# New keys' probabilities turned with the cached keys' instead of by a TensorE transpose, in an fp32 attention kernel on one core

## The chip, the core and the metric

The kernel runs on one core of a Trainium2 chip. The metric is the device time of one execution in microseconds. All arithmetic is in fp32. A core has TensorE (PE in the profile; PEld is its weight load, which overlaps the matmuls), VectorE (DVE), ScalarE (ACT), GpSimd (POOL) and SyncE (SP), each with its own instruction queue worked off in order, and 16 DMA engines.

## The reference

Four stages change a residual stream x of 32 sequences x 32 tokens x 512; the last is paged attention, and the change lies in it:

```python
x = x + L0(x, ...)   # per-sequence 32x32 mixing of tokens
x = x + L1(x, ...)   # a linear layer with a per-sequence LoRA
x = x + L2(x, ...)   # a per-sequence 512x512 linear layer
# L3: grouped-query attention, 32 query heads, 8 key heads, head size 128
k_all = concat([k_cache[block_table], k])   # 512 cached keys + the sequence's 32 new ones
scores = einsum(q, k_all) * SCALE           # cached keys at or past cache_seqlens masked
o = einsum(softmax(scores), v_all)
x = x + einsum(o, Wo)
```

## The kernel before, in words

The first part of the kernel, about a third of the time, computes L0 to L2, the projections, norms and rotations. The rest is one loop over 256 units (`for n in range(N + LAG)`), a unit being one sequence b (32) and one key head g (8), with `n = 8 b + g`. A unit is a 128-row problem: 4 query heads of the group x 32 tokens on the partitions, 544 keys (512 cached, 32 new) along the free axis. Four units make a quad, two quads (q = 0 and 1) a sequence. "Step" below means n modulo 8, counted 0 to 7; sequence b's scores are made in its own eight steps.

The order on all five engines is the order of the code (`manual_schedule`). Each step issues, in this order:

- `scores` (L1019, L1020): two pairs of matmuls on TensorE into `s_ps`, of which there is **one** buffer; then VectorE adds the mask, scales, and takes the row's minimum in one custom instruction (L1028, with an accumulator read after it), which frees `s_ps`.
- `exponentials` (L1044): ScalarE, in place in `pr` (128 x 544 for each unit, a tile for each quad), with the row sum read out after it.
- `flip_kept` (L1154): a finished quad's output is transposed by VectorE in 32x32 blocks into `ot`, one step after it was kept, but in one case in eight later (the fourth element of `kept`).
- `place`, four steps behind: the probabilities of a whole quad must be turned so that keys lie on the partitions. At step 4q + 4 + j VectorE transposes 32-column blocks of all four units at once (L1057, 128x512, into `turned`); then four copies, each from 32 partitions to 32 others (32x512), put the blocks where a 128-key chunk wants them in `placed`. ScalarE makes two of the four copies, or three in the last step of a second quad (L1069). The rest go to POOL for first quads (L1071, steps 4 to 7) and to VectorE for second quads (L1073, steps 0 to 3 of the next sequence), but for sequence 0, where POOL makes them. Two `turned` and two `placed` tiles exist.
- The new keys' 32 columns go another way. POOL gathers them from the four units in `gather_new` (L1080), at the step with j = 0; TensorE transposes the 128x128 result against the identity matrix in `flip_new` (L1084), at j = 2; ScalarE copies it out of PSUM (L1086).
- `share` (L1174): a share of the output projection of an earlier group of four sequences (a token tile t): one matmul of 128x512 (two instructions in the trace) for each unit of `SHARE`, a list of how many to issue in each of 32 steps, which starts at step 5. `LAST` is the list for the last but one tile, and takes its first 14 entries from `SHARE`. After the 32nd, VectorE adds the residual (L1183), and the projection's one PSUM buffer can be used for the next tile.
- `values`, eight steps behind (L1097): four matmuls of 128 keys into `o_ps`. After unit 3, `new_values` (L1117) adds the new keys' part for the whole sequence in eight small matmuls, and `keep` (L1131, L1133) divides the quad's output by the row sums on VectorE. After unit 7, `keep` follows for the second quad.
- After step 7, `see_keys` (L218) makes the next sequence's mask on VectorE.

Output tiles share PSUM banks: `o_ps` has one bank for each u (a unit's place in its quad), with q = 0 in its first quarter and q = 1 in its second.

Of the kernel before, what the change touches and what calls it, by code (L numbers as in the profile page):

```python
# [12 lines left out]
F32 = mybir.dt.float32  # L13
# [7 lines left out]
P = 128  # L21
B, S, HID = 32, 32, 512
D, HQ, HK = 128, 32, 8
REP = HQ // HK
PAGES, PSIZE, NPP = 64, 32, 16
L = NPP * PSIZE
# [12 lines left out]
QUAD = 4  # L39
AHEAD = 8  # L40
VS_BUFS = 2
LATE = 12
N_LOW = 9


C_BT, C_SEQ, C_TOK, C_LAB, C_COND = 0, 128, 160, 168, 176
# [13 lines left out]
def cond_resid_kernel(  # L60
# [18 lines left out]
    nc = tc.nc  # L79
# [35 lines left out]
    ident = const.tile([P, P], F32, name="ident")  # L115
# [106 lines left out]
    def load_new_keys(b: int):  # L222
        nc.sync.dma_start(out=kts[b][:, NPP, :], in_=k_d[b])
# [672 lines left out]
    tp = turn.enter_context(tc.tile_pool(name="a_t", bufs=1))  # L896
# [99 lines left out]
    ps_p = ctx.enter_context(tc.tile_pool(name="b_p", bufs=1, space=PSUM, side="right"))  # L996
# [5 lines left out]
    tp = ctx.enter_context(tc.tile_pool(name="b_t", bufs=2, side="right"))  # L1002
# [3 lines left out]
    dens, prs, pos = {}, {}, {}  # L1006
    first = L - N_LOW * PSIZE

# [3 lines left out]
    def scores(b: int, g: int):  # L1012
# [5 lines left out]
        q = qt[:, u * REP * S : (u + 1) * REP * S]  # L1018
        nc.tensor.matmul(ps[:, first:L], q, kt4[:, :N_LOW, g, :], start=True, stop=True)  # L1019
        nc.tensor.matmul(  # L1020
            ps[:, L : first + LT], q, kt4[:, N_LOW:, g, :], start=True, stop=True
        )
# [27 lines left out]
    placed = {}  # L1050

    def place(b: int, q: int, j: int):
        if j == 0:
            placed[b, q] = tp.tile([P, QUAD, L // P, P], F32, tag="placed", name=f"placed_{b}_{q}")
        pr = prs[b, q][:, :, :L].rearrange("p u (c j s) -> p j u c s", j=P // S, s=S)[:, j]
        part = tp.tile([P, QUAD, L // P, S], F32, tag="turned", name=f"turned_{b}_{q}_{j}")
        nc.vector.transpose(part, pr)  # L1057

        on_pool = q == 0 or b == 0
        if b == 0:  # L1060
            on_act = 1 + q
        else:
            on_act = 3 if q == 1 and j == QUAD - 1 else 2
        for i in range(P // S):
            dst = placed[b, q][j * S : (j + 1) * S, :, :, i * S : (i + 1) * S]
            src = part[i * S : (i + 1) * S]
            dst, src = (a.rearrange("p u c s -> p (u c) s") for a in (dst, src))
            if i < on_act:
                nc.scalar.copy(dst, src)  # L1069
            elif on_pool:  # L1070
                nc.gpsimd.tensor_copy(dst, src)  # L1071
            else:
                nc.vector.tensor_copy(dst, src)  # L1073

    pqs, pns = {}, {}

    def gather_new(b: int, q: int):

        pqs[b, q] = tp.tile([P, QUAD, S], F32, tag="pq", name=f"pq_{b}_{q}", bufs=1)
        nc.gpsimd.tensor_copy(pqs[b, q], prs[b, q][:, :, L:])  # L1080

    def flip_new(b: int, q: int):
        pnp = ps_p.tile([P, P], F32, tag="p", name=f"pn_ps_{b}_{q}")
        nc.tensor.transpose(pnp, pqs.pop((b, q)).rearrange("p u s -> p (u s)"), ident)  # L1084
        pns[b, q] = tp.tile([P, P], F32, tag="pn", name=f"pn_{b}_{q}")
        nc.scalar.copy(pns[b, q], pnp)  # L1086

    def values(b: int, g: int):

        vt = vts[b]  # L1090
        q, u = divmod(g, QUAD)
        if g == 0:
            pos[b] = ps_o.tile([P, QUAD, L], F32, tag="o", name=f"o_ps_{b}")
        po = pos[b][:, u, q * D : (q + 1) * D]
        pt = placed[b, q][:, u, :, :]
        for c in range(L // P):
            nc.tensor.matmul(  # L1097
                po,
                pt[:, c, :],
                vt[:, c, g * D : (g + 1) * D],  # L1100
                start=(c == 0 and q == 0),
                stop=(c == L // P - 1 and q == 1),
            )
        if u == QUAD - 1:
            if q == 0:
                new_values(b)
            placed.pop((b, q)), prs.pop((b, q))
            keep(b, q)

    def new_values(b: int):  # L1110

        vn = vns[b]
        for q in range(HK // QUAD):
            pn = pns.pop((b, q))
            for i in range(QUAD):
                r = slice(i * S, (i + 1) * S)
                nc.tensor.matmul(  # L1117
                    pos[b][:, i, q * D : (q + 1) * D],
                    pn[r, :],
                    vn[r, q, :],  # L1120
                    start=(q == 1),
                    stop=(q == 0),
                )

    kept = []

    def keep(b: int, q: int):

        po = pos[b] if q == 0 else pos.pop(b)
        rden = tp.tile([P, QUAD], F32, tag="rden", name=f"rden_{b}_{q}")  # L1130
        nc.vector.reciprocal(rden, dens.pop((b, q)))  # L1131
        o = tp.tile([P, QUAD * D], F32, tag="os", name=f"os_{b}_{q}")
        nc.vector.tensor_tensor(  # L1133
            o.rearrange("p (u d) -> p u d", d=D),
            po[:, :, q * D : (q + 1) * D],
            rden.unsqueeze(2).to_broadcast([P, QUAD, D]),
            ALU.mult,
        )


        at = BT * HK * (b // BT) + LAG + HK + QUAD - 2 if (b % BT, q) == (0, 1) else 0
        kept.append((b, q, o, at))
# [60 lines left out]
    LAG = 8  # L1203

    SHARE = [1, 1, 2, 1, 1, 1, 1, 1, 2, 1, 1, 1, 1, 1] + [1, 1, 0] + [1] * 7 + [0] + [1] * 7

    LAST = SHARE[:14] + [1, 1, 0, 1, 0, 1, 1, 1, 1, 1, 0, 1, 0] + [1, 1, 1, 2, 2]
    BEGIN = BT * HK + LAG - QUAD + 1  # L1210

    def share(n: int):
        t, i = divmod(n - BEGIN, BT * HK)
        if 0 <= t < NT - 1:
            parts = LAST if t == NT - 2 else SHARE
            done = sum(parts[:i])
# [4 lines left out]
    units = [(b, g) for b in range(B) for g in range(HK)]  # L1221
# [25 lines left out]
    with tc.manual_schedule(engines=order):  # L1247
        for n in range(N + LAG):
            b, g = divmod(n, HK)
            if n == FILLED + 2:  # L1250
                pa.close()
                late = ctx.enter_context(tc.tile_pool(name="b_w", bufs=1))
                places.append(late)
                wos[1] = late.tile([P, LATE, HID], F32, name="wo_1")
            if BEGIN <= n <= N and n % (BT * HK) == 0:

                load_residual((n - BEGIN) // (BT * HK))
            if n < N:
                if g == 0 and b >= 1:
                    load_queries(b, 1)  # L1260
                if g == 0 and 1 <= b < B - 1:
                    load_keys(b + 1)
                    load_new_keys(b + 1)
                    keys.dsts = page_keys(b + 1)
                    keys.transfer(slice(0, 12))
                if g < L // P and b >= 2:
                    load_value_chunk(b, g)
                if g == QUAD and b < B - 1:
                    load_queries(b + 1, 0)
                    load_inverses(b + 1)  # L1270
                    if b >= 1:
                        keys.transfer(slice(12, NPP))
                    if 1 <= b < B - 2:
                        load_table(b + 2)
                if g == QUAD + 1 and b >= 1:
                    load_new_values(b)
                if g == QUAD + 2 and b < B - 2:
                    keys = Picked(nc.sync, k_cache, pages_of.pop(b + 2), range(NPP), K_SHAPE)
                scored = scores(b, g)
                exponentials(*scored)  # L1280
            flip_kept(n)
            fill(n)
            if n in unstored:
                store_values(*unstored.pop(n))
            if n == QUAD + 1:
                load_new_values(0)
            if n in WO_AT:
                load_wo(2 * WO_AT.index(n))
            if QUAD <= n < N + QUAD:
                bq, i = divmod(n - QUAD, HK)  # L1290
                q, j = divmod(i, QUAD)
                if j == 0:
                    gather_new(bq, q)
                if j == 2:
                    flip_new(bq, q)
                place(bq, q, j)
            share(n)
            if n >= LAG:
                values(*units[n - LAG])
            if n < N and g == HK - 1 and b < B - 1:  # L1300
                see_keys(b + 1)
            if n > N + QUAD:
                at = 4 * (n - N - QUAD - 1)
                finish(NT - 1, range(at, at + 4))
        assert not dens and not prs and not pos and not placed and not pns
        load_residual(NT - 1)
        flip_kept(N + LAG)
        finish(NT - 1, range(3 * QUAD, HALF))
        finish_by_halves(NT - 1)
# [76 lines left out]
```

## Time and profile before

| | |
|---|---|
| median of 3 runs | 1142.0 us (1140.49 to 1142.26) |
| profiled execution | 1139.8 us, of which the span is 1138.0 us |
| granted TensorE clock | 1.0 |
| TensorE's L1097 / L1174 | 270.4 / 241.3 us busy |
| VectorE's L1028 / L1057 / L1073 | 200.6 / 178.7 / 94.6 us busy |
| ScalarE's L1069 / L1044 | 332.8 / 192.2 us busy |
| POOL's L1071 | 163.6 us busy |
| TensorE's L1084 (the transposes in question) | 64 of 273 ns, 17.4 us busy |

A line of the profile names the engine, the line of the kernel, the operation, the tiles written and read, and their shapes as partitions x elements; a line by shape ends with the count, the busy time, the mean of one in ns and the idle time ahead. In a timeline the first column is the start in us from the span's beginning and the second the length; neighbours of one kind are merged and counted (x2), and a bracket tells how long the engine had been idle, and for what. Matmuls overlap in the pipeline, so that what one costs is the distance of starts, not its length.

### The profile page before, as it was taken

Reading aid. Unit: us, or ns where it says so; the run is one execution under the profiler, and the core shown is the slowest. Engines: PE = TensorE matmul, PEld = TensorE weight load, DVE = VectorE, ACT = ScalarE, POOL = GpSimd, SP = SyncE. Lnnn points to the kernel's source line nnn. Section 1 sums busy time; section 2 is a strip of 40 time slices with the busy share of each in tenths; the row PEclk is TensorE's granted clock in tenths of the full one; section 3 lists DMA queues with packets and bytes.
Section 4 is the critical chain, followed back from the end, with each engine's and each line's share of the span. In section 5 each row is a group of like instructions: output and inputs, shape, how many; then the busy total and the mean of one; then the engine's idle time right before and its main releaser. Section 6 shows DMA issues by size and latency. Waiting matters only on the chain. (4 is left out here: it accounts for less than half of the span.)

```text
span 1138.0 us, 18994 instructions
## 1 busy us (share of the span) xinstructions
PE 1122.4 (99%) x5432; PEld 730.1 (64%) x5432; DVE 807.5 (71%) x1670; ACT 752.8 (66%) x1900; POOL 559.0 (49%) x719
## 2 busy tenths in 40 slices
PE   8999999999999999999999999999999999999998
PEld 5554444444444577777777777777777777777766
DVE  2510688886977487777778868877877777877851
ACT  1211377576666688777777777877777877777750
POOL 3411689899897544533443344334533443344310
PEclk9999999999999999999999999999999999999999
DMA  8998447688786587888667756765776676766610
GB/s 319 392 419 347 176 133 220 174 234 229 197 232 169 159 272 267 271 308 284 216 217 243 248 190 230 262 229 178 243 251 223 200 239 224 240 202 214 222 29 10
DMA packets 173354, 259.24 MB, mean 228 GB/s; under 512 B 31522, under 2 KB 130466, under 8 KB 168770
## 3 DMA queue, kind: packets, MB, share of 16 engines
q1 hardware_dynamic: 152226, 184.22, 51.0%
q0 software_dynamic: 20016, 71.97, 17.7%
q10 hardware_dynamic: 1008, 1.84, 0.4%
q8 instruction: 44, 0.72, 0.3%
q14 instruction: 60, 0.49, 0.1%
HBM read 228.46 MB, written 37.88 MB: 234 GB/s over the span
## 5 line engine op out<-in xcount | busy, mean ns | idle before, releaser
L1069 ACT COPY placed<-turned 32x512 f32<-32x512 f32 x539 | 332.8, 617 | 31.4 <-DVE turned L1057 24.0
L1097 PEld LDWEIGHTS o_ps<-vt,placed 128*128 128x128 f32 x2048 | 267.0, 191 | 118.5 <-issue 89.4
L1028 DVE CUSTOM_DVE_ANT_0 pr<-s_ps,mask,rq 128x544 f32<-128x544 f32 x256 | 200.6, 784 | 132.5 <-PE s_ps L1020 124.0
L1044 ACT ACTIVATE pr<-pr,low 128x544 f32<-128x544 f32 x256 | 192.2, 751 | 132.7 <-DVE low L1028 130.8
L1071 POOL COPY placed<-turned 32x512 f32<-32x512 f32 x268 | 163.6, 611 | 230.8 <-DVE turned L1057 164.1
L1097 PE MATMUL o_ps<-vt,placed 128*128 128x128 f32 x2048 | 270.4, 275 | 5.6 <-ACT placed L1069 2.8
L1174 PE MATMUL f_ps<-wo,ot 128*128 128x512 f32 x480 | 241.3, 594 | 0.7
L1057 DVE STREAM_TRANSPOSE turned<-pr 128x512 f32<-128x512 f32 x256 | 178.7, 698 | 0.1
L1019 PE MATMUL s_ps<-kt,qt 128*128 128x288 f32 x512 | 174.4, 422 | 1.4 <-DVE low L1028 0.5
L1020 PE MATMUL s_ps<-kt,qt 128*128 128x256 f32 x512 | 152.3, 379 | 0.4 <-issue 0.4
L252 POOL DMA_INDIRECT vt<-in_v_cache_dram,v_idx x128 | 128.0, 1000 | 36.6 <-issue 25.4
L1020 PEld LDWEIGHTS s_ps<-kt,qt 128*128 128x128 f32 x512 | 97.2, 190 | 27.5 <-DMA kt<-in_k_cache_dram 0.8
L434 POOL TENSOR_TENSOR ra<-ra,rs 128x512 f32<-128x512 f32 x80 | 103.9, 1306 | 10.6 <-DVE rs L429 6.4
L1174 PEld LDWEIGHTS f_ps<-wo,ot 128*128 128x128 f32 x480 | 85.8, 190 | 28.6 <-issue 13.9
L1073 DVE COPY placed<-turned 32x512 f32<-32x512 f32 x217 | 94.6, 436 | 5.5
L1080 POOL COPY pq<-pr 128x128 f32<-128x128 f32 x64 | 18.6, 290 | 149.4 <-PE o_ps L1097 94.6
L447 ACT ACTIVATE sq<-x 128x128 f32<-128x128 f32 x256 | 76.4, 302 | 19.3 <-DVE x L405 13.9
L1019 PEld LDWEIGHTS s_ps<-kt,qt 128*128 128x128 f32 x512 | 77.3, 191 | 17.0 <-DVE low L1028 10.6
L544 ACT COPY r<-m 128x512 f32<-128x512 f32 x80 | 46.4, 580 | 52.4 <-PE m L389 51.4
L389 PE MATMUL m<-t_pair,x_sums 128*128 128x512 f32 x160 | 75.3, 593 | 0.6 <-ACT r L544 0.6
L389 PE MATMUL m<-w_pair,x3t 128*128 128x512 f32 x160 | 75.2, 592 | 0.0
L389 PE MATMUL m<-w_pair,x_sums 128*128 128x512 f32 x160 | 72.1, 592 | 0.0
(129 smaller groups left out, 1223.6 us busy)
## 6 DMA issues: line engine op xcount, KB each, us to landing
kt<-in_k_cache_dram SPq DMA_DIRECT2D x512, 128.0 KB
wa<-in_w_adapt_dram SPq DMA_DIRECT2D x32, 1024.0 KB
q_d<-st SPq DMA_DIRECT2D x128, 128.0 KB
qt<-q_d SPq DMA_DIRECT2D x64, 256.0 KB
w_pair<-in_w_qkv_dram SPq DMA_DIRECT2D x20, 512.0 KB
o_d<-in_w_o_dram SPq DMA_DIRECT2D x16, 512.0 KB
wo<-o_d SPq DMA_DIRECT2D x16, 512.0 KB
k_d<-st SPq DMA_DIRECT2D x32, 128.0 KB
```

The costliest lines, as they stand in the source:

```text
L252: nc.gpsimd.indirect_dma_start(out=vts[b][:, c, :], out_offset=None, in_=v_cache, in_offset=bass.IndirectOffsetOnAxis(ap=v_idx[:, at : at ...
L389: nc.tensor.matmul(ps, of[:, k], by[:, k], start=(not more and k == 0), stop=(k == KH - 1), skip_group_check=more,)
L434: nc.gpsimd.tensor_tensor(u.a, u.a, u.s, ALU.add)
L1019: nc.tensor.matmul(ps[:, first:L], q, kt4[:, :N_LOW, g, :], start=True, stop=True)
L1020: nc.tensor.matmul(ps[:, L : first + LT], q, kt4[:, N_LOW:, g, :], start=True, stop=True)
L1028: nc.vector.tensor_tensor_reduce(pr, ps[:, first : first + LT], mask, rqs[b][:, g // QUAD, u : u + 1], 3.0e38, ALU.add, ALU.min, low,)
L1044: nc.scalar.activation(pr, pr, AF.Exp, bias=low, scale=-1.0, accum_out=dens[quad][:, u : u + 1])
L1057: nc.vector.transpose(part, pr)
L1069: nc.scalar.copy(dst, src)
L1071: nc.gpsimd.tensor_copy(dst, src)
L1097: nc.tensor.matmul(po, pt[:, c, :], vt[:, c, g * D : (g + 1) * D], start=(c == 0 and q == 0), stop=(c == L // P - 1 and q == 1),)
L1174: nc.tensor.matmul(pfs[t][:, :HID], ots[t, h // HALF][:, h % HALF, :], wo(h), start=(h == 0), stop=(h == (HQ if t < NT - 1 else HALF) - 1),)
```

## The change

`placed` and `turned` become 17 blocks wide in place of 4 x 4: the seventeenth (index `NEW`) holds the new keys. `place` issues a second, small VectorE transpose, 128x32, of unit j's new-key columns into it, and its four copies carry 17 blocks (544 elements). With j as the unit and j as the row block, four steps leave the new keys' probabilities of unit u in rows 32u to 32u + 31, as `new_values` wants them. `gather_new` and `flip_new` go.

VectorE's copies (the last branch in `place`) now run with columns outermost: both operands are seen as 32 columns x 17 blocks, so that neighbours in the stream are 128 words apart in `placed` and 32 words apart in `turned`. ScalarE's and POOL's copies keep blocks outermost.

`new_values` needs both quads' `placed` tiles, and the second is ready only after step 3; so it is issued in step 4 ahead of `values` of unit 4, where it was at the end of step 3. `keep` of the first quad follows those `values`. With the keep, the flip of a first quad comes a step later too (step 5 for step 4), and the share that would have used it at once is moved: `SHARE` begins with 0, 2 in place of 1, 1.

```diff
+NEW = QUAD * (L // P)
     def place(b: int, q: int, j: int):
         if j == 0:
-            placed[b, q] = tp.tile([P, QUAD, L // P, P], F32, tag="placed", name=f"placed_{b}_{q}")
+            placed[b, q] = tp.tile([P, NEW + 1, P], F32, tag="placed", name=f"placed_{b}_{q}")
         pr = prs[b, q][:, :, :L].rearrange("p u (c j s) -> p j u c s", j=P // S, s=S)[:, j]
-        part = tp.tile([P, QUAD, L // P, S], F32, tag="turned", name=f"turned_{b}_{q}_{j}")
-        nc.vector.transpose(part, pr)
+        part = tp.tile([P, NEW + 1, S], F32, tag="turned", name=f"turned_{b}_{q}_{j}")
+        nc.vector.transpose(part[:, :NEW].rearrange("p (u c) s -> p u c s", u=QUAD), pr)
+        nc.vector.transpose(part[:, NEW], prs[b, q][:, j, L:])
...
         for i in range(P // S):
-            dst = placed[b, q][j * S : (j + 1) * S, :, :, i * S : (i + 1) * S]
+            dst = placed[b, q][j * S : (j + 1) * S, :, i * S : (i + 1) * S]
             src = part[i * S : (i + 1) * S]
-            dst, src = (a.rearrange("p u c s -> p (u c) s") for a in (dst, src))
             if i < on_act:
                 nc.scalar.copy(dst, src)
             elif on_pool:
                 nc.gpsimd.tensor_copy(dst, src)
             else:
+                dst, src = (a.rearrange("p u s -> p s u") for a in (dst, src))
                 nc.vector.tensor_copy(dst, src)
-    def gather_new(b: int, q: int):
-        pqs[b, q] = tp.tile([P, QUAD, S], F32, tag="pq", name=f"pq_{b}_{q}", bufs=1)
-        nc.gpsimd.tensor_copy(pqs[b, q], prs[b, q][:, :, L:])
-    def flip_new(b: int, q: int):
-        pnp = ps_p.tile([P, P], F32, tag="p", name=f"pn_ps_{b}_{q}")
-        nc.tensor.transpose(pnp, pqs.pop((b, q)).rearrange("p u s -> p (u s)"), ident)
-        pns[b, q] = tp.tile([P, P], F32, tag="pn", name=f"pn_{b}_{q}")
-        nc.scalar.copy(pns[b, q], pnp)
     def values(b: int, g: int):
-        pt = placed[b, q][:, u, :, :]
+        pt = placed[b, q][:, u * (L // P) : (u + 1) * (L // P), :]
...
-        if u == QUAD - 1:
-            if q == 0:
-                new_values(b)
+        if g == HK - 1:
             placed.pop((b, q)), prs.pop((b, q))
             keep(b, q)
     def new_values(b: int):
-            pn = pns.pop((b, q))
+            pn = placed[b, q][:, NEW, :]
...
+        placed.pop((b, 0)), prs.pop((b, 0))
-    SHARE = [1, 1, 2, 1, 1, 1, 1, 1, 2, 1, 1, 1, 1, 1] + [1, 1, 0] + [1] * 7 + [0] + [1] * 7
+    SHARE = [0, 2, 2, 1, 1, 1, 1, 1, 2, 1, 1, 1, 1, 1] + [1, 1, 0] + [1] * 7 + [0] + [1] * 7
...
-                if j == 0:
-                    gather_new(bq, q)
-                if j == 2:
-                    flip_new(bq, q)
                 place(bq, q, j)
             share(n)
             if n >= LAG:
+                if units[n - LAG][1] == QUAD:
+                    new_values(units[n - LAG][0])
                 values(*units[n - LAG])
+                if units[n - LAG][1] == QUAD:
+                    keep(units[n - LAG][0], 0)
```

## The prediction

> **What bounds the kernel now.** I read the page first, for the busiest engine, then the timeline of one sequence in mid-run, then the costs by line and shape. The page:
>
> ```profile
> PE 1122.4 (99%) x5432; PEld 730.1 (64%) x5432; DVE 807.5 (71%) x1670; ACT 752.8 (66%) x1900; POOL 559.0 (49%) x719
> ```
>
> TensorE (PE) is busy almost throughout, so removed TensorE work can show in the time, if nothing takes its place. The span is 1138.0 us, the profiled execution 1139.8, the median of the runs 1142.0: I sum against 1139.8 and add 2.2 for the median.
>
> The timeline of sequence 15 shows what the 99% hides. Columns: start us, length us, engine, line, operation.
>
> ```profile
> 706.24 0.65 PE L1019 MATMUL s_ps<-kt,qt 128*128 128x288 f32 x2
> ...
> 707.05 0.69 DVE L218 TENSOR_SCALAR mask<-key_i,len_f 128x544 f32<-128x544 int16 x1
> ...
> 707.87 0.78 DVE L1028 CUSTOM_DVE_ANT_0 pr<-s_ps,mask,rq 128x544 f32<-128x544 f32 x1
> ...
> 708.58 0.70 DVE L1154 STREAM_TRANSPOSE ot<-os 128x512 f32<-128x512 f32 x1
> ...
> 708.91 0.65 PE L1019 MATMUL s_ps<-kt,qt 128*128 128x288 f32 x2
> ...
> 709.21 0.67 DVE L1057 STREAM_TRANSPOSE turned<-pr 128x512 f32<-128x512 f32 x1
> ...
> 709.91 0.88 DVE L1073 COPY placed<-turned 32x512 f32<-32x512 f32 x2
> ...
> 710.82 0.78 DVE L1028 CUSTOM_DVE_ANT_0 pr<-s_ps,mask,rq 128x544 f32<-128x544 f32 x1
> ...
> 711.67 0.75 PE L1019 MATMUL s_ps<-kt,qt 128*128 128x288 f32 x2
> ...
> 712.69 0.27 PE L1084 MATMUL pn_ps<-ident,pq 128*128 128x128 f32 x1
> ...
> 712.80 1.02 PE L1174 MATMUL f_ps<-wo,ot 128*128 128x512 f32 x2
> ...
> 717.31 0.73 PE L1117 MATMUL o_ps<-vn,pn 32*128 32x128 f32 x16
> 717.37 1.88 ACT L1069 COPY placed<-turned 32x512 f32<-32x512 f32 x3
> ```
>
> Call S the start of a step's L1019, and L the start of its L1028 on VectorE. The score tile has one buffer, so the next S waits for L: 710.82 to 711.67, S = L + 0.85. L in turn follows the scores by at least 1.12. Undisturbed, S to S is 2.67 (706.24 to 708.91); here 2.76, because VectorE has the mask, a flip and two copies in its queue and its L is late. So steps 0 to 3 of a sequence, where the second quad is placed with VectorE's copies, already stand at VectorE's edge: its own step there is 2.95 with the flip (707.87 to 710.82) and 2.33 without, against TensorE's 2.67. In steps 4 to 7 POOL copies instead, and VectorE waits.
>
> **What is removed.** 64 transposes on TensorE. Each is 273 ns long, but 712.69 to 712.80 is 0.11: the next matmul starts over its tail. So 64 x 0.11 = 7.0 us on the path, not 17.4. ScalarE's 64 copies (245 ns) and POOL's 64 (290 ns) lie beside the path, at nothing. The Trainium skill ("TensorE: Matmul & The Clock Gate", Part 4: PE-mode transpose) has about 275 ns for a transpose inside a kernel; the duration agrees, and by it the gain would be 64 x 0.275 = 17.6 us, but the start-to-start time in this trace decides.
>
> **What is added to VectorE's steps.** The prices, from the costs by shape:
>
> ```profile
> L1073 DVE COPY placed<-turned 32x512 f32<-32x512 f32 x217 | 94.6, 436 | 5.5
> ...
> L468 DVE TENSOR_REDUCE ss<-x 128x4 f32<-128x512 f32 x16 | 10.6, 662 | 0.0
> ...
> L714 DVE TENSOR_REDUCE low<-picked 128x32 f32<-128x160 f32 x8 | 3.5, 443 | 0.5
> ...
> L643 DVE TENSOR_REDUCE quarter<-ident 128x4 f32<-128x128 f32 x1 | 0.3, 277 | 0.0
> ```
>
> A transpose of 128x32, 256 of them: a 512-column one takes 0.63 start to start (708.58 to 709.21); 480 columns fewer at 1.00 ns (662 less 277 over 384 elements) leave 0.15. Bounds: 0.08 (the accumulator read, VectorE's smallest row) to 0.70.
>
> VectorE's copies, 217 of 32x544. Contiguous, 436 x 544/512 = 463 ns, the lower bound. But with columns outermost each element is read 32 words and written 128 words after the one before. The row nearest to that is L714, a sum that also steps 32 words: 160 elements contiguous would be 277 + 32 = 309 ns, it takes 443, so 1.84 ns an element instead of 1.00. The present copy (436 for 512) must move two elements at once; I assume that it still does: 272 x 1.84 = 500, plus 436 - 256 = 180 fixed, 0.68 us. Upper bound, one at a time: 544 x 1.84 + 150 = 1.15 us. I take 0.68, nearest to the row; losing the pairs but not paying for the steps would give about the same (544 + 150 = 0.69). The Trainium skill ("VectorE: DVE Perf Modes", What auto-detection actually checks) lets a copy use both ports if the outermost dimensions are even, or equal; 17 blocks on both sides are equal, so by it the new order buys nothing and 0.46 was to be had without it. No run here shows that; it would give the first rival's sum.
>
> So each tight step with two copies grows by 0.15 + 2 x 0.24 = 0.63 us.
>
> **Step by step**, for the kind of sequence shown (two in four; before 2.67, 2.76, 2.88, 3.42, 2.77 us from S0 to S5). L0 = S0 + 1.63 as now, since there the keep waits for TensorE anyway. L1 = L0 + 2.95 + 0.63 = S1 + 2.54, so S2 = S1 + 3.39. Then VectorE's 2.33 + 0.63 = 2.96 is the step: S3 and S4 2.96 each. S4 comes without the new values (they took 0.75 of step 3).
>
> In step 4 the new values now wait for the second quad's last copies. ScalarE begins them 1.70 after L3 (exponential, 717.37 - 715.67) and needs three of 627 + 26 ns: L3 + 3.66, that is S4 + 2.81. TensorE would be at the last new-value matmul at S4 + 2.55: a share starts 1.02 after a delayed S (712.69 to 711.67, the transpose's place) and lasts 0.86, then 0.09 and seven eighths of the new values' 0.66. With 0.25 for the release and the weight load and 1.07 for that matmul and the four of L1097, S5 = S4 + 4.13. Behind this wait in TensorE's queue stand the values of step 4 and S5; VectorE's keep waits for those, so moving it there costs nothing: it ends 0.75 after them, before TensorE next needs the banks (0.92).
>
> Sum 16.11 against 14.50: +1.61, less 0.11 for step 6's transpose: +1.50. The two other kinds, sequences 17 and 18, with their own starts (L0 at 1.43: 2.67, 3.19, 3.05, 2.96, 4.13 against 14.30; flip in step 2: 2.67, 2.96, 3.15, 3.63, 4.13 against 14.30) give +1.59 and +2.13. POOL's two copies of step 7 begin 0.15 later and last 2 x 26 ns longer; TensorE reads them with at most 0.12 to spare, so 0.1 a sequence (bounds 0 to 0.2). The SHARE edit takes away a wait of 0.38 per token tile (step 5 of 3.05 against 2.67, L1174 behind L1183) and makes a step without a share, whose S waits 0.26: -0.12. Four sequences: 2 x 1.50 + 1.59 + 2.13 + 0.40 - 0.12 = +7.0 us. VectorE copies in 30 sequences, the first two of them partly covered by waits for keys: 29/4 x 7.0 = +51 us. So 1139.8 + 51 = 1191, and 1193 by the median.
>
> The wider tiles cost ScalarE 26 ns a copy, elsewhere beside the path. The first placed tile lives one step longer; its third user, step 4's first copies, starts about 1.75 after the scores and the new values end about 1.6 after: nothing, but 0.2 if late. No DMA is added or moved.
>
> **Rivals.**
> - *Copies at their present rate* (0.46): each tight step grows by 0.19. The same walk gives +0.18, +0.18, +0.27 and +0.81, with POOL and SHARE +1.7 per four: 29/4 x 1.7 = +12, 1154 us. For it: nothing in the trace shows a copy with such steps. Against: L714. Chance 0.22, with 1146 to 1170.
> - *Copies one element at a time* (or a new transpose near its upper bound, +49): +1.57 a step, first kind 2.67, 4.33, 3.90, 3.90, 4.13 and so +4.3, x 29 = +125, 1267 us. Against: the halves stay even (32 columns). 0.06.
> - *Faster*: VectorE's growth hides and TensorE keeps its saving, 7.0 + 0.8 from SHARE: 1134 us. It decides where a tight step grows by less than about 0.1: then the stall of step 1 and ScalarE's wait together are below 0.22 a sequence. For it: VectorE is idle for 0.2 to 1.4 us before L1028 in the other steps, and the first quad's keep has left step 3. Against: step 1 already stalls by 0.09, and the new transpose alone is 0.15. 0.13. *Cancelled*, within 0.2% (about what a measurement here can tell): 0.07.
>
> **Numbers.** Forecast 0.52, 1193. Between 0.19 and 0.63 a tight step lie 39 us, so 89 us for each us; copies of 0.57 to 0.82 us make 0.41 to 0.87 a step, the forecast's own range 1173 to 1215. Faster 0.13, same 0.07, slower 0.52 + 0.22 + 0.06 = 0.80. The range, 1138 to 1215, leaves out the faster case and the 1267 one.
>
> **What the changed profile would show.** The copies' mean near 680 ns against 436; the small transposes near 0.15; in steps 1 to 3 S to S of 3.0 to 3.4 with TensorE's weight load waiting for L1028; in step 4 the new values waiting for ScalarE. TensorE's share falls to some 95%. Copies near 460 ns make the forecast wrong towards 1154; a tight step that stays at 2.67 makes it wrong in sign.

## The result and the profile after

The changed kernel takes 1187.55 us (median, 1187.14 to 1188.54), the kernel before beside it 1141.67: ratio 1.0404, 95% interval 1.0391 to 1.0418. It is 45.9 us slower; the forecast was 51 us slower. The profiled span is 1186.8 us, against 1138.0.

The page's line of engine shares: TensorE has 64 instructions less and is idle for 37.9 us of the span in place of 15.6, but its busy time rose by 26.5 us too. So a busy TensorE in this record is not TensorE at work, and the steps have to be read, not the share.

```profile
PE 1148.9 (97%) x5368; PEld 735.9 (62%) x5368; DVE 876.5 (74%) x1926; ACT 752.6 (63%) x1836; POOL 554.3 (47%) x655
```

The costs by line and shape (count, then busy us and mean ns) have the two disputed prices: 647 ns a copy where 680 was forecast, and 169 ns for the small transpose.

```profile
L1075 DVE COPY placed<-turned 32x544 f32<-32x544 f32 x217 | 140.5, 647 | 5.5
...
L1059 DVE STREAM_TRANSPOSE turned<-pr 128x32 f32<-128x32 f32 x256 | 43.4, 169 | 0.0
...
L219 DVE TENSOR_SCALAR mask<-key_i,len_f 128x544 f32<-128x544 int16 x32 | 23.6, 739 | 0.0
```

The timeline of sequence 15, steps 0 to 4, to be laid beside the one before (L1020 is what L1019 was, L1029 what L1028 was):

```profile
728.72 0.65 PE L1020 MATMUL s_ps<-kt,qt 128*128 128x288 f32 x2
...
728.74 1.32 POOL L1072 COPY placed<-turned 32x544 f32<-32x544 f32 x2 [1.35 <-DVE rden L1119]
...
729.53 0.83 DVE L219 TENSOR_SCALAR mask<-key_i,len_f 128x544 f32<-128x544 int16 x1
...
730.49 0.78 DVE L1029 CUSTOM_DVE_ANT_0 pr<-s_ps,mask,rq 128x544 f32<-128x544 f32 x1
...
731.39 0.70 PE L1020 MATMUL s_ps<-kt,qt 128*128 128x288 f32 x2
731.83 0.67 DVE L1058 STREAM_TRANSPOSE turned<-pr 128x512 f32<-128x512 f32 x1
...
732.43 0.17 DVE L1059 STREAM_TRANSPOSE turned<-pr 128x32 f32<-128x32 f32 x1
732.63 1.29 DVE L1075 COPY placed<-turned 32x544 f32<-32x544 f32 x2
...
733.95 0.78 DVE L1029 CUSTOM_DVE_ANT_0 pr<-s_ps,mask,rq 128x544 f32<-128x544 f32 x1
...
734.66 0.71 DVE L1058 STREAM_TRANSPOSE turned<-pr 128x512 f32<-128x512 f32 x1
...
734.80 0.75 PE L1020 MATMUL s_ps<-kt,qt 128*128 128x288 f32 x2 [0.52 <-issue]
...
735.49 1.28 DVE L1075 COPY placed<-turned 32x544 f32<-32x544 f32 x2
...
736.81 0.78 DVE L1029 CUSTOM_DVE_ANT_0 pr<-s_ps,mask,rq 128x544 f32<-128x544 f32 x1
...
737.65 0.75 PE L1020 MATMUL s_ps<-kt,qt 128*128 128x288 f32 x2
...
740.56 0.75 PE L1020 MATMUL s_ps<-kt,qt 128*128 128x288 f32 x2
...
741.41 1.95 ACT L1070 COPY placed<-turned 32x544 f32<-32x544 f32 x3
...
742.53 0.72 PE L1104 MATMUL o_ps<-vn,placed 32*128 32x128 f32 x14
...
743.40 0.48 PE L1104 MATMUL o_ps<-vn,placed 32*128 32x128 f32 x2 [0.15 <-ACT placed L1070]
```

From step 1 on, each S now comes 0.85 after the L before it: 733.95 to 734.80, 736.81 to 737.65. Between two L lie 2.86 us of VectorE's own work, where TensorE needs 2.67. At the end 14 of the 16 new-value instructions run, and the last two wait for ScalarE's third copy, which ends at 743.36. The steps, S to S in us, from timelines:

| | step 0 | 1 | 2 | 3 | 4 | 5 | 6 | 7 | four sequences |
|---|---|---|---|---|---|---|---|---|---|
| before, sequence 19 | 2.67 | 2.75 | 2.88 | 3.42 | 2.77 | 1.97 | 2.88 | 2.67 | 90.97 |
| forecast for it | 2.67 | 3.39 | 2.96 | 2.96 | 4.13 | | | | 98.0 |
| after, sequence 19 | 2.67 | 3.40 | 2.88 | 2.90 | 4.26 | 1.97 | 2.77 | 2.66 | 96.84 |

### The profile page after: what moved, and what is told of

The parts are those of the page before. It is cut to its first block, busy times and chain, and to the rows that moved or that the text cites. A ratio compares the mean times of both kernels' runs of the same rounds, so it can differ in the third digit from the quotient of the medians.

```text
span 1186.8 us, 19001 instructions
## 1 busy us (share of the span) xinstructions
PE 1148.9 (97%) x5368; PEld 735.9 (62%) x5368; DVE 876.5 (74%) x1926; ACT 752.6 (63%) x1836; POOL 554.3 (47%) x655
## 3 DMA queue, kind: packets, MB, share of 16 engines
q0 software_dynamic: 20016, 71.97, 16.9%
q10 hardware_dynamic: 1008, 1.84, 0.4%
## 5 line engine op out<-in xcount | busy, mean ns | idle before, releaser
L1070 ACT COPY placed<-turned 32x544 f32<-32x544 f32 x539 | 346.2, 642 | 36.8 <-DVE turned L1059 20.7
L1072 POOL COPY placed<-turned 32x544 f32<-32x544 f32 x268 | 170.1, 635 | 426.8 <-DVE rden L1119 221.0
L1086 PEld LDWEIGHTS o_ps<-vt,placed 128*128 128x128 f32 x2048 | 263.9, 191 | 107.8 <-issue 78.7
L1086 PE MATMUL o_ps<-vt,placed 128*128 128x128 f32 x2048 | 276.0, 278 | 4.7 <-ACT placed L1070 1.7
L1029 DVE CUSTOM_DVE_ANT_0 pr<-s_ps,mask,rq 128x544 f32<-128x544 f32 x256 | 200.5, 783 | 82.3 <-PE s_ps L1021 73.1
L1020 PE MATMUL s_ps<-kt,qt 128*128 128x288 f32 x512 | 180.6, 434 | 17.3 <-DVE low L1029 10.5
L253 POOL DMA_INDIRECT vt<-in_v_cache_dram,v_idx x128 | 135.7, 1060 | 39.8 <-issue 29.5
L1075 DVE COPY placed<-turned 32x544 f32<-32x544 f32 x217 | 140.5, 647 | 5.5
L1162 PEld LDWEIGHTS f_ps<-wo,ot 128*128 128x128 f32 x480 | 90.6, 190 | 27.3 <-issue 17.2
L1020 PEld LDWEIGHTS s_ps<-kt,qt 128*128 128x128 f32 x512 | 76.9, 189 | 40.6 <-DVE low L1029 24.0
L1121 DVE TENSOR_TENSOR os<-o_ps,rden 128x512 f32<-128x512 f32 x64 | 44.2, 691 | 63.5 <-PE o_ps L1086 63.3
```

The costliest lines, as they stand in the source:

```text
L253: nc.gpsimd.indirect_dma_start(out=vts[b][:, c, :], out_offset=None, in_=v_cache, in_offset=bass.IndirectOffsetOnAxis(ap=v_idx[:, at : at ...
L1029: nc.vector.tensor_tensor_reduce(pr, ps[:, first : first + LT], mask, rqs[b][:, g // QUAD, u : u + 1], 3.0e38, ALU.add, ALU.min, low,)
L1086: nc.tensor.matmul(po, pt[:, c, :], vt[:, c, g * D : (g + 1) * D], start=(c == 0 and q == 0), stop=(c == L // P - 1 and q == 1),)
L1162: nc.tensor.matmul(pfs[t][:, :HID], ots[t, h // HALF][:, h % HALF, :], wo(h), start=(h == 0), stop=(h == (HQ if t < NT - 1 else HALF) - 1),)
```

## The experiments

Theory: the time goes where VectorE's longer copies and the small transposes stretch the tight steps, and where the new values wait for ScalarE. Rivals: the moved new values alone; 17 blocks or the wider tile as such; TensorE's saving never worth 0.11 each. The kernels ran in three groups, each beside the kernel before on its own chip. There it took 1139.94 us (blocks outermost, halves outermost, columns alone, TensorE's transpose twice), 1142.08 (rows apart, last copy shared, flip in slack, small transpose twice) and 1139.84 (the two with the mask first). All differences are to that.

### 1. The order of VectorE's copies

Three kernels are the changed one with another order; the first drops the line that puts columns outermost, the other two are:

```diff
# halves outermost
-                dst, src = (a.rearrange("p u s -> p s u") for a in (dst, src))
+                dst, src = (a.rearrange("p u (h s) -> p h u s", h=2) for a in (dst, src))
# blocks outermost, source rows apart
-                dst, src = (a.rearrange("p u s -> p s u") for a in (dst, src))
-        part = tp.tile([P, NEW + 1, S], F32, tag="turned", ...)
+        part = tp.tile([P, NEW + 1, S + 2], F32, tag="turned", ...)[:, :, :S]
```

> The changed kernel with VectorE's copies blocks outermost again (17 x 32, runs of 32 adjacent words). Theory (the price of the copies is the single-word steps, and most of the loss is theirs): if the copy keeps moving two elements at once, 463 ns a copy, a tight step grows by 0.09 + 0.04 = 0.13 us over before, and the time is about 1151 (before + 9; the wait of the new values for ScalarE in step 4 stays). Rival (17 is odd, so the copy loses its two-element rate whatever the order, and columns outermost is the cheaper of two evils): about 544 + 150 = 690 to 720 ns a copy and 1190 to 1200 us. Rival (the copies hardly matter, the moved new values do): 1180 or more whatever the copies take.

> The changed kernel with VectorE's copies as 2 halves of 16 columns outermost, then 17 blocks, then 16 adjacent words: an even outermost count and no single-word steps. Theory: 463 ns a copy and about 1151 us, whether or not the odd 17 costs the rate. Rival (17 blocks or the wider tile are dear in themselves): above 600 ns and above 1180 us. Rival (copies hardly matter): 463 ns, but 1180 or more.

> Blocks outermost as in the run of that name, but with the rows of turned 34 words apart, so that the 17 source blocks don't touch and can't be read as one run of 544. If the lost two-element rate came of 17 on one side against 544 (merged) on the other, the copies fall from 711 ns to about 435 and the time to about 1150. If an odd outermost count alone loses it, they stay near 711 ns and 1199 us.

Blocks outermost: 1199.4 us, +59.5 (ratio 1.0522, 1.0505 to 1.0540). Halves outermost: 1149.56, +9.6 (1.0087, 1.0071 to 1.0104). Rows apart: 1156.97 in a single run, +14.9. Their rows for the copies, one kernel after the other:

```profile
L1074 DVE COPY placed<-turned 32x544 f32<-32x544 f32 x217 | 154.3, 711 | 5.5
```

```profile
L1075 DVE COPY placed<-turned 32x544 f32<-32x544 f32 x217 | 94.5, 435 | 5.5
```

```profile
L1074 DVE COPY placed<-turned 32x544 f32<-32x544 f32 x217 | 97.8, 451 | 5.5
```

The theory of the first run (463 ns, 1151 us) failed, and its rival's numbers came: 17 blocks outermost do lose the two-element rate. That 711 ns is one element at a time is worked out, not seen: it is 276 ns above the 435 of halves, about 1 ns for each of the 272 elements that no longer go along with another. Columns outermost saved 64 ns of that. But the price was that of the order alone: in halves, the same 544 elements take 435 ns, and the change loses 9.6 us in place of 45.9. Two rivals fall, that of 17 or the wider tile as such and that of copies that hardly matter. That the gap of two words between rows brings the rate back too speaks for the reading that rows of `turned` which touch count as one run of 544, which is not the 17 of the other side; what merges them was not seen. The Trainium skill ("VectorE: DVE Perf Modes", What auto-detection actually checks) has a copy use both ports if the outermost dimensions are both even, or equal. With 17 on both sides the run with the gap agrees with that (451 ns), and the run without it does not (711 ns), unless its source counts as one run. The 5 us between the last two kernels come mostly from one sequence in four, whose steps 3 and 4 are 3.09 and 4.26 against 2.67 and 4.12; why stays open.

### 2. Columns outermost as the only edit to the kernel before

```diff
             else:
+                dst, src = (a.rearrange("p u s -> p s u") for a in (dst, src))
                 nc.vector.tensor_copy(dst, src)
```

> The kernel before with columns outermost in VectorE's copies as the only edit (16 blocks). Theory: the changed kernel's 647 ns less 180 fixed is 1.72 ns for each of 272 pairs, so 256 of them make 620 ns; a tight step grows by 0.37 us, and the walk through the steps gives +3.0 us per four sequences, about 1164 us (before + 22). Rival (copies hardly matter; moved new values and small transposes do): copies of 620 ns, but 1142 to 1148 us.

1156.79 us, +16.9 (1.0149, 1.0132 to 1.0166); copies of 615 ns.

```profile
L1074 DVE COPY placed<-turned 32x512 f32<-32x512 f32 x217 | 133.5, 615 | 5.5
```

The mechanism stands; the size is below the 22 expected. Four sequences take 93.03 us, 2.06 more than before, where the expectation had 3.0. In sequence 19 step 1 grew by 0.38 and step 4 by 0.14; in the sequence whose flip is in step 2, step 4 alone grew, to 3.46. Taken off the changed kernel, the same order is worth 36 us (45.9 less 9.6). There, in sequence 19, steps 1 to 4 lose 0.40, 0.11, 0.23 and 0.52 by it (3.00, 2.77, 2.67 and 3.74 with halves), against 0.38, 0, 0 and 0.14 here. Step 3 shows why the two differ: in the kernel before the new values keep TensorE busy there (3.42, with and without the new order), so that longer copies hide; in the changed kernel they have gone to step 4, and VectorE has the small transposes besides. How much each of these two adds was not taken apart.

### 3. TensorE's transpose issued twice, in the kernel before

```diff
-        nc.tensor.transpose(pnp, pqs.pop((b, q)).rearrange("p u s -> p (u s)"), ident)
+        pq = pqs.pop((b, q)).rearrange("p u s -> p (u s)")
+        for _ in range(2):
+            nc.tensor.transpose(pnp, pq, ident)
```

> The kernel before with each TensorE transpose of the new keys issued twice into the same PSUM tile, so 64 more. Theory (start-to-start price): +0.11 us each, 7 us, about 1149 us. Rival (each costs its length): +0.273 each, 17.5 us, about 1159 us. No change at all would mean that the removal was worth nothing.

1145.68 us, +5.7 (1.0051, 1.0034 to 1.0067, so 3.9 to 7.6 us). 7.0 lies in the interval, 17.5 doesn't. In the timeline the projection starts 0.22 after the first of the pair, 0.11 each:

```profile
714.97 0.38 PE L1086 MATMUL pn_ps<-ident,pq 128*128 128x128 f32 x2
...
715.19 1.02 PE L1176 MATMUL f_ps<-wo,ot 128*128 128x512 f32 x2
```

### 4. The small transpose issued twice

```diff
# on top of halves outermost
-        nc.vector.transpose(part[:, NEW], prs[b, q][:, j, L:])
+        for _ in range(2):
+            nc.vector.transpose(part[:, NEW], prs[b, q][:, j, L:])
```

> Halves outermost, with VectorE's small transpose of the new keys issued twice into the same block. Theory (it costs VectorE 0.10 us start to start, and in tight steps that is passed on, to step 1 and through ScalarE's copies to step 4): about +0.3 us a sequence, +9 us over the run with halves alone, 1158 us. Rival (hidden in VectorE's slack): 1150 us. If its length counted (169 ns): some 1164 us.

1184.07 us, +42.0, which is 32.4 more than the +9.6 of halves alone, far from all three numbers. This measures something else: the second writes what the first wrote, and the pair takes 0.45 from start to copy where one takes 0.20 (732.43 to 732.63 in the changed kernel). The second begins at 731.00, after the first has ended (730.97), where the first begins ahead of the end of the large transpose (730.80 against 730.88); so it waits, most likely for the block that it overwrites.

```profile
728.71 1.13 PE L1087 MATMUL o_ps<-vt,placed 128*128 128x128 f32 x8
...
728.87 0.78 DVE L1029 CUSTOM_DVE_ANT_0 pr<-s_ps,mask,rq 128x544 f32<-128x544 f32 x1
...
729.72 0.75 PE L1020 MATMUL s_ps<-kt,qt 128*128 128x288 f32 x2
...
730.80 0.41 DVE L1060 STREAM_TRANSPOSE turned<-pr 128x32 f32<-128x32 f32 x2
...
731.25 0.88 DVE L1076 COPY placed<-turned 32x544 f32<-32x544 f32 x2
```

It is no price for one transpose. It does show where VectorE has slack left: 0.25 us more in each step makes a sequence like number 19 longer by 0.20, 0.30, 0.0, 0.04 and 0.55 in steps 0 to 4, so there is some in steps 2 and 3 and next to none in the others. In step 0 POOL's copies come so late that TensorE's values start 1.86 after S0 in place of 1.78; that is the wait that the forecast had put at 0.1 for the change. But the 0.20 are VectorE's: L0 comes 2.02 after S0, behind the mask, and S again 0.85 after it (728.87 to 729.72).

### 5. What is left after the copies: step 4, the flip, the mask

Each of the first two kernels adds an edit to the one before it, from halves outermost on; the third moves the mask in the second of them, the fourth in the kernel before.

```diff
# last copy shared: ScalarE two copies instead of three in a second quad's last step
-            on_act = 3 if q == 1 and j == QUAD - 1 else 2
+            on_act = 2
# flip in slack
-        at = BT * HK * (b // BT) + LAG + HK + QUAD - 2 if (b % BT, q) == (0, 1) else 0
+        at = HK * b + 2 * HK + QUAD if q == 1 and b < B - 1 else 0
# mask first
             share(n)
+            if n < N and g == HK - 1 and b < B - 1:
+                see_keys(b + 1)
             if n >= LAG:
...
-            if n < N and g == HK - 1 and b < B - 1:
-                see_keys(b + 1)
```

> Halves outermost, and ScalarE makes two copies instead of three in a second quad's last step (VectorE the other two). Theory (what is left of the loss sits mostly in step 4, where the new values wait for ScalarE's third copy): ScalarE is done 0.65 us earlier, step 4 falls from 3.74 and 4.12 us to about 3.5, that is 1.3 us per four sequences, about 1140 us. Rival (step 4 is long for another reason, the restart of TensorE's weight loads behind the small matmuls): step 4 stays 3.74, only one sequence in four gains 0.4, about 1146 us.

> The run before this one, and the second quads' flips put off to step 4 of the sequence after next, out of the tight steps. Theory (VectorE's step 0 with flip, two copies and the small transpose still exceeds TensorE's 2.67 us and delays step 1): steps 1 and 2 fall from 2.99 and 2.77 us to 2.67, about 1.0 us per four sequences, so about 7 us less than the run before, near 1133 us, below both kernels. Rival (TensorE's removed transposes were never worth their 0.11 us each): no less than 1140 us.

> The version with the second quads' flips put off, and the next sequence's mask made ahead of the second quad's keep in step 7 instead of behind it, so that VectorE makes it while it waits for TensorE's values. Theory (in three of four sequences L0 comes 1.77 us after S0 and costs 0.05 in step 1, and with it goes a wait of 0.2 to 0.3 in step 2 that the sequence with L0 at 1.43 doesn't have): L0 falls to about 1.4, steps 1 to 3 to 2.67 each, about 1.0 us per four sequences and 7 us in all, 1133 us. Rival (the wait in step 2 has another cause, such as what POOL does there): steps 2 and 3 stay 2.85 and 2.77, 1139 us.

> The kernel before with the same move of the mask as its only edit. Theory: L0 falls from 1.63 us to about 1.3, step 1 of every second sequence from 2.76 to 2.67 and its 0.1 in step 2 goes, 0.4 us per four sequences, 3 us, 1139 us. If it gains as much as the run beside it, that one's gain over the kernel before is the mask's and not the removed transposes'.

| kernel | median us | to before | ratio, 95% interval | four sequences, us |
|---|---|---|---|---|
| halves outermost | 1149.56 | +9.6 | 1.0087 (1.0071 to 1.0104) | 91.83 |
| last copy shared | 1144.04 | +2.0 | 1.0017 (1.0008 to 1.0027) | 91.29 |
| flip in slack | 1140.43 | -1.7 | 0.9987 (0.9977 to 0.9996) | 90.91 |
| mask first | 1134.74 | -5.1 | 0.9950 (0.9937 to 0.9963) | 89.72 |
| before, mask first | 1136.71 | -3.1 | 0.9970 (0.9959 to 0.9982) | 90.59 |

Sharing the last copy brought step 4 from 3.74 and 4.12 to 3.52 and 3.62, as the theory of the wait for ScalarE had it; the time missed 1140, since in one sequence in four steps 2 and 3 grew from 2.67 to 2.87 and 3.05. Moving the flip took step 1 from 3.00 to 2.72, but a wait ahead of L2 now lengthened step 2 in three sequences of four, and 1133 became 1140. That is the number of the rival (the removed transposes worth nothing), but the doubled transposes above and the last two rows of the table speak against it. In the timeline of the flip's kernel VectorE has finished its copies at 714.63 and the scores of step 2 end at 714.45, and still L1029 waits:

```profile
713.75 0.88 DVE L1075 COPY placed<-turned 32x544 f32<-32x544 f32 x2
713.86 0.59 PE L1021 MATMUL s_ps<-kt,qt 128*128 128x256 f32 x2
...
715.39 0.78 DVE L1029 CUSTOM_DVE_ANT_0 pr<-s_ps,mask,rq 128x544 f32<-128x544 f32 x1 [0.76 <-PE s_ps L1021]
```

What it waits for is not in the trace, and stays open. The sequence without this wait was the one whose L0 came early, and with it POOL's gathers of cached values (L253). In sequence 22, where these gathers start 1.8 us later than elsewhere, L2 comes without a wait too, 6.69 us after S0 in place of 7.33 to 7.43; but with halves the same gathers lie beside the same copies, and there is no wait, so the gathers alone don't make it. With the mask ahead of the keep L0 falls from 1.77 to 1.14, L1 to L3 come right behind the scores, for which VectorE waits some 0.24 after its copies, and all four steps are 2.67:

```profile
704.53 0.88 DVE L1075 COPY placed<-turned 32x544 f32<-32x544 f32 x2
...
705.64 0.78 DVE L1029 CUSTOM_DVE_ANT_0 pr<-s_ps,mask,rq 128x544 f32<-128x544 f32 x1 [0.23 <-PE s_ps L1021]
...
707.19 0.88 DVE L1075 COPY placed<-turned 32x544 f32<-32x544 f32 x2
707.19 0.65 PE L1020 MATMUL s_ps<-kt,qt 128*128 128x288 f32 x2
...
708.31 0.78 DVE L1029 CUSTOM_DVE_ANT_0 pr<-s_ps,mask,rq 128x544 f32<-128x544 f32 x1 [0.24 <-PE s_ps L1021]
```

That is the fastest version, below both kernels (1133 was expected, and 1139 by the rival). The mask's move alone gives the kernel before 3.1 us, as expected, so not all of the gain is the change's. Between the two by four sequences lie 0.87 us, as much as eight transposes of 0.11 (0.88); steps 2 and 6 of sequence 19 are 2.67 and 2.77 against 2.78 and 2.88. For 29 sequences that would be 6.3 us. By medians it is only 2.0, with intervals that overlap from 0.9959 to 0.9963, but the six runs of the one (1131.15 to 1135.37) all lie below the six of the other (1135.66 to 1137.91). Two of the six, the profiled one among them, take some 1131 us and four some 1135; why is open.

## Why the prediction was right

Point by point, by its own steps.

- *The path.* S = L + 0.85 behind steps 1 to 3 in sequences 15 to 19, as forecast, and the step is VectorE's. Right. (TensorE's share of busy time is 97%, where the prediction had some 95%.)
- *TensorE's transposes*: 0.11 each, not 0.273. Right (runs of the doubled transpose and of the last table).
- *The copies*: 0.68 forecast, 0.647 measured, 5% high. The row it was taken from, a sum that steps 32 words, gave 1.84 ns for each element; with the forecast's fixed part (647 - 180) / 272 = 1.72 is what the copy pays for each pair. But from 512 to 544 elements the copy grew by 32 ns (615 to 647), 2.0 for each of 16 pairs, so that split isn't settled, and the prediction itself had another way to 0.69, with the pairs lost. For pairs speaks that 647 lies below 711. The size is right, its reason is argued; that a row of another operation came so near is in part luck.
- *Copies of 0.46 with blocks outermost*, which the prediction read off the skill's rule: wrong, they take 711 ns (first run).
- *The range*: by the prediction's own rule copies of 0.82 us make 0.92 a step, not 0.87, and the upper end 1219, not 1215. The result lies inside both.
- *The small transpose*: 0.15 forecast. From the large transpose's start to the copies' it is 0.83 now (734.66 to 735.49) and was 0.74, so 0.09. With the copies, VectorE's step is 2.86 against 2.33, +0.53 for +0.63. This is the mis-sized term: for four sequences the forecast has steps 1 to 3 1.2 us too long and POOL's wait 0.4, and step 4 0.5 too short, which together is what lies between 98.0 and 96.84 us. So the sequences lose 5.87 us in four for a forecast 7.0, which is 42.6 us in all; another 1.1 is a longer end (from the last unit's S to the end of the span 49.68 against 48.58), which the forecast had not. That part of these errors cancel is luck.
- *The new values' wait for ScalarE*: forecast on the last matmul; 14 of 16 instructions ran and two waited. Step 4 is 4.26 for 4.13: right, slightly low.
- *Where the first rival would have been right*: with copies at 435 ns it walked to +12 us; the run with halves gave +9.6.
- *L0 unchanged at 1.63*: it is 1.77, since the mask takes 0.83 in place of 0.69 (last section). Wrong, by 0.14.
- *POOL's late copies*, +0.1 a sequence: wrong, step 0 stays 2.67.
- *The SHARE edit*, -0.12 for four sequences: steps 5 to 7 of sequence 16 go from 9.36 to 9.12, of which 0.11 is the transpose's. Right.
- *The keep behind the values of unit 4 costs nothing*: step 5 without a share stays 1.97. Right.

So of the 45.9 us, taken off in this order, some 36 are the order of VectorE's copies, 5 to 8 the wait in step 4 (1149.56 to 1144.04, or +9.6 to +2.0), and 4 the flip in a step that has no room for it. TensorE's saving (7.0 us by starts, 5.7 by the doubled transposes) is in all of them.

## What to carry to other kernels

When one engine is at 99%, look at which of its steps are already paced by another: what is taken from the first engine counts at its distance of starts, and what is put on the second counts in just those steps, as far as the first engine leaves it no slack there. An access order is part of an instruction's price: before changing it for one rule, look for a split that keeps runs of adjacent words as well, and time that copy by itself. And when a producer is moved onto a longer route, walk the new last arrival (here ScalarE's third copy) against the consumer's new place.

## What the runs showed of the hardware

The mask, one VectorE instruction of 544 elements, takes 464 ns at its shortest, but 690 in the median of the kernel before and 832 after, where it lies beside POOL's copies; where it starts ahead of them it takes 461 (in the lines: shortest, median, longest; kernel before, changed kernel, mask first):

```profile
L218 DVE TENSOR_SCALAR mask<-key_i,len_f x32: 464/690/857, 36.0 to 1070.8; 128x544 f32<-128x544 int16 x32
```

```profile
L219 DVE TENSOR_SCALAR mask<-key_i,len_f x32: 461/832/908, 36.7 to 1117.0; 128x544 f32<-128x544 int16 x32
```

```profile
L219 DVE TENSOR_SCALAR mask<-key_i,len_f x32: 459/461/502, 36.7 to 1060.6; 128x544 f32<-128x544 int16 x32
```

In sequence 15 the mask starts 0.39 us before POOL's second copy ends in the kernel before, and 0.53 in the changed one (729.53 against 730.06); it is longer than 461 ns by 0.23 and by 0.37. Where the mask starts first, POOL's pair of copies is the longer one, 1.50 us against 1.31:

```profile
699.21 1.31 POOL L1072 COPY placed<-turned 32x544 f32<-32x544 f32 x2 [0.17 <-DVE turned L1059]
...
701.74 0.46 DVE L219 TENSOR_SCALAR mask<-key_i,len_f 128x544 f32<-128x544 int16 x1
...
701.88 1.50 POOL L1072 COPY placed<-turned 32x544 f32<-32x544 f32 x2 [1.35 <-DVE turned L1059]
```

The Trainium skill ("SBUF — State Buffer", Who interferes with whom) says that VectorE in a two-port mode and GpSimd exclude each other for an instruction's length, and that the one that starts first goes on. The runs agree in that the later of the two is the longer one each time; they show neither the lock itself nor that the mask runs in such a mode.
